# A fixed program order by kinds of matmul, and a new slot check, in a two-layer graph network on one core

## The chip, the core and the metric

The kernel runs on one core of a Trainium2 chip. The core has a matrix engine (PE; its weight loads are listed as PEld), a vector engine (DVE), a scalar engine (ACT), a general engine (POOL) and a queue that starts transfers (SP). Each engine executes its own instructions in the order in which the program issued them, and waits where one needs another engine's result or a buffer that is still read. The metric is the device time of one execution in microseconds (us); less is better.

## What is computed

128 graphs of 128 nodes with 64 features go through two layers, each followed by a residual sum and a layer norm. The reference, cut to what matters:

```python
def layer0(x, adj, W1, b1, W2, b2):          # W1 is 128 x 192, W2 is 192 x 64
    mask = (adj > 0.0)
    diff = x[:, :, None, :] - x[:, None, :, :]
    h = relu((x @ W1[:64])[:, :, None, :] + diff @ W1[64:] + b1)
    hm = einsum('bjkh,bjk->bjh', h, mask)    # sum over the neighbours k of j
    return hm @ W2 + mask.sum(-1)[..., None] * b2

def layer1(feat, adj, W1, b1, W2, b2, W3, b3):
    agg = einsum('bmn,bnd->bmd', adj, feat)
    return elu(elu(agg @ W1 + b1) @ W2 + b2) @ W3 + b3

x = layernorm(x + layer0(x, adj, ...))
x = layernorm(x + layer1(x, adj, ...))
```

The adjacency has few neighbours per node, so layer 0 visits neighbours and not all pairs of nodes.

## The kernel before

Graphs are handled in 64 pairs. In each pair the nodes are sorted by their number of neighbours. The sorted nodes fall into nine BLOCKS (first row, last row, slots): the 18 nodes of rows 65 to 83, for instance, get 9 slots each, which makes 162 columns. A node of block i must not have more neighbours than the block has slots; a check at the end of the kernel (overflow, L792) finds pairs for which that fails, and a dense path then does them again. For this input no pair needs it.

For each pair the work is a set of threads, Python generators whose every step names an engine, a cost, what it waits for, and how many of four shared PSUM banks (m0 to m3) it takes:

- prepare (L527): count the neighbours (DVE L536), make keys (POOL), spread them over rows (PE L549, L551), compare and rank (DVE L558), build a permutation (DVE L565).
- turn (L674): transpose adj and x (PE L680, L681) into one bank, copy it out as turned (ACT L685). project_c (L690) multiplies by weights (PE L698, L701) and splits the result into three bf16 parts cp (ACT, DVE L712, ACT L715, POOL L717).
- sort_x (L574) and project_a: sort x (PE L582), copy (ACT L586), multiply (PE L596), add the bias (ACT L603, gives aj), and a correction for short nodes: POOL L610, PE L616 and L619 (short), DVE L625, POOL L632.
- sort_mask (L635): sort the mask (PE L641, L644), copy it (ACT L649 mtp, L651 permT), count along a row (PE L655, prefix; ACT L658), and compare with slot numbers in nine pieces (DVE L665), which gives oh.
- unit, nine for a pair: copy aj into an edge bank (ACT L882; four edge banks e0 to e3, taken in turn), gather with 18 matmuls of a 64-column stationary side (PE L894), reduce over slots (DVE L903, gives sums).
- finish (L805): take off the correction (POOL L812, gives hm), project (PE L817, L821, L824), copy as ys (ACT L828), a small transfer of the degrees ys[128:130] to degs (SP L830), unsort (PE L836), norm, aggregate over neighbours (PE L843, ACT L847), hidden1 (PE L852), elu, hidden2 (PE L858), elu, last (PE L863, L865), norm, transfer out.

The class Flow (L88) writes the program order. It keeps a clock for each engine, and takes again and again the step that could start first; among steps of that engine that could start nearly as early (NEAR, NEAR_PE) it takes the one with the earliest due time. Due times are written out in DUE, relative to the start of a pair's round (ROUND times the pair's number). A step has a mode behind a colon: "PE:t" is work whose stationary side has 64 columns. A change of mode costs SWITCH on Flow's clock. Flow's clock only decides the order; it is no time of the chip. A unit also may not start, on that clock, before T0 + pace(u).

So the order of a period comes out of a list of dues and a rule that looks at readiness, and repeats itself from pair to pair once it has settled: one period of PE has nine gathers (L894) in five groups, and between them the steps of other pairs' threads.

Of the kernel before, what the change touches and what calls it, by code (L numbers as in the profile page):

```python
# [87 lines left out]
class Flow:  # L88
# [8 lines left out]

    LAG = 0.2
    NEAR = 0.1
    NEAR_PE = 0.03  # L100
    SWITCH = 0.1
    HOLD = 0

    def __init__(self, banks):
        self.clock = {}
        self.threads = []
        self.free = [(0.0, b) for b in banks]
        self.serial = 0
        self.mode = ""

# [35 lines left out]

    def _switch(self, engine, mode):
        return self.SWITCH if engine == "PE" and mode != self.mode else 0.0

    def _rank(self, th):  # L150
        engine, _, mode = th[4][0].partition(":")
        return th[0] + (self.HOLD if self._switch(engine, mode) else 0.0), th[1]

    def run(self):
        while self.threads:
            ready = [(t, th) for t, th in ((self._ready(th[4]), th) for th in self.threads)
                     if t is not None]
            t, th = min(ready, key=lambda r: (r[0], r[1][0], r[1][1]))
            first = th[4][0].split()[0].partition(":")[0]
            near = t + (self.NEAR_PE if first == "PE" else self.NEAR)  # L160
            t, th = min((r for r in ready if r[1][4][0].split()[0].partition(":")[0] == first
                         and r[0] <= near), key=lambda r: self._rank(r[1]))
            engine, cost, after, banks, fn = th[4]
            args = []
            if banks:
                self.free.sort(key=lambda f: f[0])
                args = [self.free.pop(0)[1] for _ in range(banks)]
            fn(*args)
            for e in engine.split():
                e, _, mode = e.partition(":")  # L170
                self.clock[e] = t + cost
                if e == "PE":
                    self.mode = mode
# [3 lines left out]
def sparse(tc, env):  # L177
# [6 lines left out]
    NE = 4  # L184
# [7 lines left out]
    ROUND = 11.14  # L192
    AHEAD = 3
    PACE = ROUND / NB

    DUE = {
        "prepare": (-34.32, -34.43, -29.25, -33.33, -26.26),
        "sort_x": (-25.05, -19.47, -20.79, -15.63, -11.78, -14.33, -11.15, -5.27, -5.97),
        "sort_mask": (-24.98, -24.21, -19.11, -17.63, -31.08, -14.67, -12.13, -9.2, -7.19, -6.42,
                      -4.21, -1.99, -12.24, -7.24),  # L200
        "turn": (-25.52, -21.42),
        "project_c": (-19.53, -25.02, -26.5, -19.03, -18.18, -16.73, -23.86),
        "finish": (7.83, 15.84, 19.72, 16.78, 21.09, 22.6, 28.99, 31.57, 29.07, 31.37, 30.6,
                   34.42, 35.7, 33.91, 37.94, 41.34, 41.72, 43.55, 44, 37.02, 51.36),
        "unit": (-1.1, 0.98, 2.36),
    }

    def pace(u):
        return PACE * u

    def begin_thread(name, p, gen):
        flow.start(ROUND * p, DUE[name], gen)

    T0 = []
# [17 lines left out]
    def pool(n):  # L232
        return 0.15 + n * 0.0022

# [31 lines left out]
    slots = const([P, 1], F32, "slots")  # L266
# [27 lines left out]
    worst = const([P, NP], F32, "worst")  # L294
    bad = const([P, NP], BF16, "bad")
    count = const([1, NP], I32, "count")
    some = const([1, 1], I32, "some")
    K = dict(count=count, some=some, ident=ident, identb=identb, onesb=onesb, mhalf=mhalf, mone=mone, slots=slots,
# [170 lines left out]
    def consts_late():  # L469
# [9 lines left out]
        def v1diag():  # L479
# [5 lines left out]
        ev, t = yield ("PE", 0.1, made("srow2", "small"), 1, lambda t: nc.tensor.matmul(  # L485
            t[:, :1], srow2, small[:, 0:1], start=True, stop=True))
        ev, = yield ("ACT", 0.2, [ev], 0, lambda: nc.scalar.copy(slots, t[:, :1]))
        flow.give(t, ev)


# [36 lines left out]
    def prepare(p):  # L527
# [4 lines left out]
        deg = prep.tile([P, 2], F32, name="deg")  # L532
# [12 lines left out]
        ev, = yield ("POOL PORT", 0.43, [ev] + made("jcol"), 0, keys)  # L545

        def spread(key):
            for s in range(2):
                nc.tensor.matmul(key[:, s * N:(s + 1) * N], degb[:, s:s + 1].to_broadcast([P, P]),  # L549
                                 identb, start=True, stop=True)  # L550
            nc.tensor.matmul(key[:, 2 * N:3 * N], small, iotb, start=True, stop=True)  # L551
        ev, key = yield ("PE", 0.17, [ev] + made("identb", "small", "iotb"), 1, spread)
# [37 lines left out]
    def project_a(p, xsT, ev):  # L590
# [19 lines left out]
        evs, = yield ("POOL PORT", 0.95, [have] + made("srow"), 0, lambda: nc.gpsimd.tensor_mul(sa, aj, srow))  # L610
# [24 lines left out]
    def sort_mask(p, ev):  # L635
# [3 lines left out]
        def sort(t):  # L639
            for s in range(2):  # L640
                nc.tensor.matmul(t[:, s * N:(s + 1) * N], d["mk"][:, s, :], permb[:, s, :],  # L641
                                 start=True, stop=True)
            for s in range(2):
                nc.tensor.matmul(t[:, (2 + s) * N:(3 + s) * N], permb[:, s, :], identb,  # L644
                                 start=True, stop=True)
        ev, t = yield ("PE", 0.22, [ev], 1, sort)
# [7 lines left out]
        ev, vps = yield ("PE", 0.11, [evm] + made("prefix"), 1,  # L654
                         lambda vps: nc.tensor.matmul(vps[:, :2 * N], prefix, flat(mtp),  # L655
                                                      start=True, stop=True))
# [17 lines left out]
    def turn(p):  # L674
# [7 lines left out]
        ev, t = yield ("PE", 0.4, [event("load", p)] + made("ident"), 1, transpose)  # L682
# [7 lines left out]
    def project_c(p, ev):  # L690
# [11 lines left out]
        ev, *cps = yield ("PE", 0.7, [ev] + made("wc", "b2p", "onesb"), 2, project)  # L702
# [19 lines left out]
    def norm(p, yps, ev, name, rest, shift):  # L722
# [29 lines left out]
        if p < LATE:  # L752
            ev, = yield ("POOL PORT", 1.24 if shift else 0.88, [ev] + made("mhalf"), 0, factors)
# [38 lines left out]
    def overflow(ev):  # L792

        v = nc.vector
        ev, = yield ("DVE", 0.25, [ev], 0, lambda: v.tensor_reduce(
# [352 lines left out]
```

## Time and profile before

| | us |
|---|---|
| Runs | 769.13 (median of 3), 766.89 to 770.3 |
| Profiled execution | 766.95 |
| Span of the profiled execution (first to last instruction) | 765.2 |
| PE busy, of the span | 746.0 |
| DVE busy | 718.6 |
| ACT busy | 700.9 |
| POOL busy | 430.7 |
| Gathers L894, 10368 matmuls | 390.8 |
| First reduce of the first pair | 23.90 after the start |
| Last reduce of the last pair starts | 746.00 after the start |

The costliest lines of the page beside the gathers are the reduces and the edge copies, each near 5 us for a pair, on DVE and on ACT:

```profile
L903 DVE TENSOR_REDUCE sums<-e 128x54 f32<-128x486 f32 (+8 forms) x576 | 330.5, 609 | 12.8 <-PE e L894 12.3
L882 ACT COPY e<-aj 128x504 f32<-128x504 f32 (+6 forms) x576 | 309.3, 558 | 7.2 <-DVE sums L903 6.8
```

A line of this kind names the line of code, the engine, the operation, output and input tiles with their shapes and the count; after the first bar stand the busy time in us and the mean of one in ns, after the second the idle time of the engine just before these instructions, and what ended most of it. Busy time on PE is not the same as work: matmuls are pipelined, and their ends are modelled. What one costs in a stream is the distance from its start to the next start.

### The profile page before, as it was taken

How to read it: one execution, taken by the hardware profiler on the slowest of the kernel's cores; microseconds unless marked ns; L12 is line 12 of the kernel's file. 1: busy time of each engine (PE TensorE's matmuls, PEld its weight loads, DVE VectorE, ACT ScalarE, POOL GpSimd, SP SyncE). 2: the span in 40 equal slices, each digit the busy share in tenths (PEclk: the TensorE clock that was granted, in tenths of full speed). 3: DMA queues.
4: the chain of work that ended last, by engine and by line, in shares of the span. 5: the costliest groups of instructions: out<-in, count | busy, mean ns of one | idle time of the engine just before them, and what ended most of it. 6: DMA issues, size and time to landing. Idle time of an engine off the chain costs nothing.

```text
span 765.2 us, 35336 instructions
## 1 busy us (share of the span) xinstructions
PE 746.0 (97%) x14487; PEld 671.7 (88%) x14488; DVE 718.6 (94%) x2363; ACT 700.9 (92%) x1987; POOL 430.7 (56%) x801
## 2 busy tenths in 40 slices
PE   7899999999999999999999999999999999999994
PEld 5688998998998999899899899899889889889893
DVE  7999999999999999999999999999999999999984
ACT  5788999999999999999999999999999999999984
POOL 6445565565665665665665665665665655655542
PEclk9999999999999999999999999999999999999998
DMA  3011110110110110110011010111011011010000
GB/s 82 3 24 27 28 30 21 27 31 19 28 30 20 28 29 21 26 31 23 25 30 27 21 31 22 26 31 30 18 31 30 18 31 31 17 30 21 9 10 18
DMA packets 63879, 19.73 MB, mean 26 GB/s; under 512 B 46816, under 2 KB 63712, under 8 KB 63712
## 3 DMA queue, kind: packets, MB, share of 16 engines
q1 hardware_dynamic: 63008, 17.12, 9.5%
q8 instruction: 115, 1.88, 1.0%
q14 instruction: 52, 0.43, 0.2%
q10 hardware_dynamic: 704, 0.30, 0.1%
HBM read 13.14 MB, written 4.19 MB: 23 GB/s over the span
## 4 chain that ended last, share of the span: by engine, by line
PE 94%; DVE 3%; ACT 2%; issue 1%; DMA 0%; ACTq 0%; POOLq 0%; POOL 0%; DVEq 0%
PE e L894 44%; PE m L596 6%; PE m L817 6%; PE m L698 5%; PE m L852 4%; PE m L858 4%; PE m L865 4%; PE m L836 3%; PE m L680 2%; PE m L582 2%; PE m L843 2%; PE m L655 2%; PE m L641 2%; PE m L821 1%; PE m L701 1%; DVE sums L903 1%
## 5 line engine op out<-in xcount | busy, mean ns | idle before, releaser
L894 PE MATMUL e<-oh,cp 128*64 128x162 bf16 (+3 forms) x10368 | 390.8, 228 | 1.8 <-ACT e L882 1.5
L894 PEld LDWEIGHTS <-cp 128*64 128x64 bf16 x10368 | 357.0, 110 | 30.6 <-issue 22.6
L903 DVE TENSOR_REDUCE sums<-e 128x54 f32<-128x486 f32 (+8 forms) x576 | 330.5, 609 | 12.8 <-PE e L894 12.3
L882 ACT COPY e<-aj 128x504 f32<-128x504 f32 (+6 forms) x576 | 309.3, 558 | 7.2 <-DVE sums L903 6.8
L665 DVE TENSOR_TENSOR oh<-vp,slotc 128x336 bf16<-128x336 bf16 (+6 forms) x576 | 168.5, 322 | 1.8 <-PE e L894 1.8
L610 POOL TENSOR_TENSOR sa<-aj,srow 128x384 f32<-128x384 f32 x64 | 65.0, 1016 | 121.0 <-ACT aj L603 118.7
L739 POOL TENSOR_SCALAR ve<-st 128x2 f32<-128x2 f32 x126 | 24.1, 192 | 160.2 <-DVE st L732 154.7
L740 POOL TENSOR_TENSOR rs<-ve,mhalf 128x2 f32<-128x2 f32 x126 | 87.6, 695 | 10.5
L717 POOL TENSOR_TENSOR cp<-r,cp 128x512 bf16<-128x512 f32 x64 | 74.1, 1158 | 13.2 <-ACT cp L715 13.2
L781 ACT ACTIVATE r<-m,cc 128x256 f32<-128x256 f32 x128 | 64.2, 502 | 4.9 <-PE m L852 3.9
L812 POOL TENSOR_TENSOR hm<-sums,corr 128x384 f32<-128x384 f32 x63 | 62.9, 999 | 8.0 <-DVE sums L903 8.0
L632 POOL TENSOR_TENSOR corr<-ea,sa 128x384 f32<-128x384 f32 x64 | 64.2, 1002 | 0.9 <-DVE ea L625 0.7
L787 DVE SCALAR_TENSOR_TENSOR h<-m,cc,e 128x256 f32<-128x256 f32 x128 | 61.1, 478 | 3.1 <-ACT e L784 3.1
L596 PE MATMUL m<-xsT,wad 128*128 128x128 f32 x384 | 58.4, 288 | 0.8 <-DVE r L712 0.6
L603 ACT ACTIVATE aj<-m,b1c 128x128 f32<-128x128 f32 x192 | 56.8, 373 | 1.0 <-PE m L596 1.0
L784 ACT ACTIVATE e<-r 128x256 f32<-128x256 f32 x128 | 57.6, 451 | 0.1
L761 ACT ACTIVATE x<-y,nb,rs 128x64 f32<-128x64 f32 x126 | 48.7, 434 | 9.1 <-POOL nb L743 8.8
L558 DVE SCALAR_TENSOR_TENSOR cmp<-m,keyc,tie 128x128 bf16<-128x128 f32 x128 | 39.9, 349 | 15.9 <-PE m L551 15.7
L817 PE MATMUL m<-w2d,hm 128*128 128x128 f32 x384 | 53.9, 277 | 0.0
L712 DVE TENSOR_TENSOR r<-m,cp 128x256 f32<-128x256 f32 x128 | 52.4, 413 | 0.8 <-ACT cp L708 0.7
L596 PEld LDWEIGHTS m<-xsT,wad 128*128 128x128 f32 x384 | 47.7, 191 | 1.9 <-DVE r L712 0.8
L817 PEld LDWEIGHTS m<-w2d,hm 128*128 128x128 f32 x384 | 48.6, 193 | 0.6
(150 smaller groups left out, 1349.5 us busy)
## 6 DMA issues: line engine op xcount, KB each, us to landing
adj<-in_adj_dram SPq DMA_DIRECT2D x64, 128.0 KB, 2.3
xx<-in_x_dram SPq DMA_DIRECT2D x64, 64.0 KB, 2.2
out_dram<-o SPq DMA_DIRECT2D x64, 64.0 KB, 1.7
degs<-ys SPq DMA_DIRECT2D x64, 1.0 KB, 1.7
w1s<-in_L_gnn_W_dram ACTq DMA_DIRECT2D x2, 96.0 KB, 2.9
w2s<-in_L_gnn_W_dram ACTq DMA_DIRECT2D x2, 48.0 KB, 2.5
v2s<-in_L_gnn_W_dram SPq DMA_DIRECT2D x1, 64.0 KB, 2.5
v1d<-in_L_gnn_W_dram SPq DMA_DIRECT2D x2, 32.0 KB, 2.1
```

What stands on the lines that cost most here:

```text
L596: nc.tensor.matmul(aps[:, c * N:(c + 1) * N], wad[:, c, :], xsT, start=True, stop=True)
L610: evs, = yield ("POOL PORT", 0.95, [have] + made("srow"), 0, lambda: nc.gpsimd.tensor_mul(sa, aj, srow))
L632: ev, = yield ("POOL PORT", 1.05, [ev, evs], 0, lambda: nc.gpsimd.tensor_sub(corr, ea, sa))
L665: lambda: nc.vector.tensor_tensor(oh[:, :, c].rearrange("p b (s w) -> p b s w", w=w), vp[:, :, p0:p1].rearrange("p b (o w) -> p b o w", o= ...
L717: lambda: nc.gpsimd.tensor_sub(cp[:, 2], r1, cp[:, 1]))
L740: nc.gpsimd.tensor_tensor(rs, ve, mhalf, op=OP.pow)
L781: lambda: nc.scalar.activation(r, z, AF.Relu, bias=c, scale=-1.0))
L812: lambda: (nc.vector if late else nc.gpsimd).tensor_sub(hm, d["sums"], d["corr"]))
L817: nc.tensor.matmul(yb[:, :2 * O], hm[:, c, :], flat(w2d[:, c]), start=(c == 0), stop=False)
L882: lambda: nc.scalar.copy(e.rearrange("p (c s w) -> p c s w", c=3, w=w), d["aj"][:, :, p0:p1].rearrange("p c (o w) -> p c o w", o=1) .to_br ...
L894: nc.tensor.matmul(e[s * HB:(s + 1) * HB, c * n:(c + 1) * n], cp[:, k, s, c * HB:(c + 1) * HB], oh[:, s, base:base + n], start=False, stop ...
L903: nc.vector.tensor_reduce(d["sums"][:, :, p0:p1], e.rearrange("p (c s w) -> p c w s", c=3, w=w), AX.X, OP.add, apply_absolute_value=True)
```

## The change

Five things are changed. A line number is that of the kernel before unless it is said otherwise; most lines of the changed kernel stand 9 to 30 lines further down.

1. *Flow* knows four kinds of matmul: "" (full array), "t" (64 columns), "r" (64 rows: L698) and "x" (transposes), and prices changes between them in a table. A kind "*" takes whatever kind is under way. From the first gather on until 14 units before the end (under_way) readiness is no longer looked at: the step with the earliest due time is next. The wait of units for T0 + pace(u) is gone.
2. *DUE* is new throughout: prepare is due 42.67 before its round and not 34.32, finish ends at 59.48 and not at 51.36, each of the nine units has dues of its own, ROUND is 11.1651. AHEAD is 4: a pair's inputs are loaded four rounds before its first unit and not three.
3. *stationary*: the matmuls of spread (L549, L551), of the sort of the mask (L641, L644) and of prefix (L655) are of kind "*". Under kind "t" each is issued as two with 64 columns of the stationary side.
4. *Degrees*: the counts of prepare go straight to degs; the two matmuls L824 for each pair, two columns of the copy ys and the transfer L830 are gone.
5. *overflow* compares the degrees with the slots of each block (nine compares), counts for each graph the rows over a limit (nine matmuls with one column of output) and compares those counts with the first row of the block. The matmul and copy that made slots (L485, L487) are gone.

In one period, PE now has four gathers (170, 162, 168, 66), project_c, last, then gather 112, short, gather 168, sort_x, gathers 154 and 169, the sort of the mask in halves, gather 154, aggregate, the transposes, spread, prefix, hidden2, project_a, project, hidden1, unsort. DVE has four reduces, elu, count, a sum, a reduce, ea, a reduce, two r, three reduces, cmp and permb, all nine compares of oh, a statistic, a sum, elu and a statistic. ACT has, between the gathers' edge copies, x, mtp, permT, agg, xsT, turned, vp in a row, then a copy, r, aj, ys, e. In the PSUM banks, the transposes and project_a of one period use the same bank (m3), with spread, prefix and hidden2 in the other three between them.

```diff
-    SWITCH = 0.1
-    HOLD = 0
+    CHANGE = {("t", ""): 0.1, ("", "t"): 0.1, ("r", "t"): 0.1, ("x", "t"): 0.1, ("", "r"): 0.1,
+              ("t", "r"): 0.1, ("x", "r"): 0.1, ("", "x"): 0.07, ("t", "x"): 0.1, ("r", "x"): 0.07}
...
+    def _kind(self, mode):
+        return mode if mode != "*" else "t" if self.mode == "t" else ""
+
     def _switch(self, engine, mode):
-        return self.SWITCH if engine == "PE" and mode != self.mode else 0.0
+        return self.CHANGE.get((self.mode, self._kind(mode)), 0.0) if engine == "PE" else 0.0
...
-            t, th = min(ready, key=lambda r: (r[0], r[1][0], r[1][1]))
-            first = th[4][0].split()[0].partition(":")[0]
-            near = t + (self.NEAR_PE if first == "PE" else self.NEAR)
-            t, th = min((r for r in ready if r[1][4][0].split()[0].partition(":")[0] == first
-                         and r[0] <= near), key=lambda r: self._rank(r[1]))
+            if self.under_way:
+                t, th = min(ready, key=lambda r: self._rank(r[1]))
+            else:
...
-    ROUND = 11.14
-    AHEAD = 3
-    PACE = ROUND / NB
+    ROUND = 11.1651
+    AHEAD = 4
...
+    def stationary(out, lhsT, rhs, **kw):
+
+        if flow.mode == "t":
+            for h in (slice(0, P // 2), slice(P // 2, P)):
+                nc.tensor.matmul(out[h], lhsT(h), rhs, **kw)
+        else:
+            nc.tensor.matmul(out, lhsT(slice(0, P)), rhs, **kw)
...
-        deg = prep.tile([P, 2], F32, name="deg")
+        deg = g.degs[:, 2 * p:2 * p + 2]
...
-        ev, key = yield ("PE", 0.17, [ev] + made("identb", "small", "iotb"), 1, spread)
+        ev, key = yield ("PE:*", 0.17, [ev] + made("identb", "small", "iotb"), 1, spread)
...
-                nc.tensor.matmul(t[:, s * N:(s + 1) * N], d["mk"][:, s, :], permb[:, s, :],
-                                 start=True, stop=True)
+                stationary(t[:, s * N:(s + 1) * N], lambda h: d["mk"][:, s, h], permb[:, s, :],
+                           start=True, stop=True)
...
-        ev, t = yield ("PE", 0.4, [event("load", p)] + made("ident"), 1, transpose)
+        ev, t = yield ("PE:x", 0.33, [event("load", p)] + made("ident"), 1, transpose)
...
-        ev, *cps = yield ("PE", 0.7, [ev] + made("wc", "b2p", "onesb"), 2, project)
+        ev, *cps = yield ("PE:r", 0.7, [ev] + made("wc", "b2p", "onesb"), 2, project)
...
+        def compare(blocks):
+            for i in blocks:
+                v.tensor_scalar(over[:, i, :], g.degs, float(BLOCKS[i][2]), None, op0=OP.is_gt)
+        for k in range(0, NB, 3):
+            ev, = yield ("DVE PORT", 0.5, [ev], 0, lambda: compare(range(k, k + 3)))
+
+        def rows_over(t):
+            for i in range(NB):
+                nc.tensor.matmul(t[:B, i:i + 1], over[:, i, :], onesb[:, 0:1], start=True, stop=True)
...
-            for s in range(2):
-                nc.tensor.matmul(yb[:, 2 * O + s:2 * O + s + 1], mtp[:, s, :], onesb[:, 0:1],
-                                 start=True, stop=True)
...
-        nc.sync.dma_start(g.degs[:, 2 * p:2 * p + 2], ys[:, 2 * O:])
...
+        flow.under_way = u < len(units) - 14
         ev, = yield ("PE:t", 0.03 + 0.0037 * n, [ev, event("cp", p), event("oh", p, i)], 0, gather)
```

## The prediction

> **What bounds the kernel now.** I read the busy times, then the stage windows, then the waits of the steady part, then one period of the timeline.
>
> ```profile
> PE 746.0 (97%) x14487; PEld 671.7 (88%) x14488; DVE 718.6 (94%) x2363; ACT 700.9 (92%) x1987; POOL 430.7 (56%) x801
> ...
> PE 94%; DVE 3%; ACT 2%; issue 1%; DMA 0%; ACTq 0%; POOLq 0%; POOL 0%; DVEq 0%
> ```
>
> Three engines look full. The windows say which one is:
>
> ```profile
> 300.00:400.00 100.00, 100.00 (x2004) 91.28 (x1998) 96.05 (x316) 95.41 (x273) 57.63 (x105) 1.00 0.11 27
> ```
>
> PE has no idle time in these 100 us, DVE and ACT have 4 to 5%. The waits between 150 and 700 us (48 periods) confirm it: no matmul is in the list as waiting for DVE, ACT or POOL, but those wait for PE. (Each line: who waits, for whom, total us, times, longest.)
>
> ```profile
> PEld L701 <- issue: 16.2, 49, 0.3
> PEld L894 <- issue: 16.2, 49, 0.3
> DVE cmp L558 <- PE m L551: 13.4, 49, 0.3
> ACT mtp L649 <- PE m L644: 11.4, 48, 0.2
> DVE sums L903 <- PE e L894: 9.4, 48, 0.2
> ```
>
> The two PEld lines are 0.3 us, once a period, in which no weights are loaded: the array changes its tiling. One period of the timeline, PE alone but for one line:
>
> ```profile
> 411.47 0.29 PE L641 MATMUL m<-permb,mk 128*128 128x128 bf16 x2
> ...
> 411.76 0.61 PE L865 MATMUL m<-v3s,h 128*128 128x64 f32 x4
> ...
> 412.30 0.70 PE L698 MATMUL m<-wc,turned 64*128 64x256 f32 x4
> ...
> 412.94 0.23 PE L701 MATMUL m<-b2p,onesb 128*128 128x64 bf16 x2
> ...
> 413.17 0.65 PE L858 MATMUL m<-h,v2s 128*128 128x256 f32 x2
> ...
> 413.75 1.48 PE L894 MATMUL e<-oh,cp 128*64 128x168 bf16 x36
> ...
> 417.66 0.91 PE L596 MATMUL m<-xsT,wad 128*128 128x128 f32 x6
> ...
> 422.90 0.28 PE L641 MATMUL m<-permb,mk 128*128 128x128 bf16 x2
> ```
>
> From L641 to L641 is 11.43 us; the first reduce of a pair comes every 11.432 us from pair 5 to pair 60. So the time is about 57 periods of 11.432 us, plus a head and a tail. The column after the tile names is the tiling: 128\*64 for gathers, 64\*128 for L698, 128\*128 otherwise.
>
> [...] L894 to L641: the last matmul of 112 columns needs 0.049 us, the next starts 0.146 us after it, so 0.097 for the drain. In the same way 0.093 at L865 to L698, 0.095 at L698 to L701, 0.093 at L858 to L894, 0.095 at L894 to L655 and 0.093 at L852 to L894. Transposes (L680) have the 128\*128 tiling: L596 to L680 costs nothing (0.112, its usual step). [...] Here an f32 load of 128 columns costs nothing behind a long matmul, but 0.104 after a drain (L817 at 724.71 took 0.377 instead of 0.275) or after a wait; 0.081 is left of it at L596, which follows the short matmuls L821 and L824.
>
> **The change on PE.** I laid the changed queue (its order is fixed by the program) out for one period, with start-to-start times of the same instructions in the trace. Gathers of 170, 162, 168 and 66 slots 0.688 + 0.634 + 0.652 + 0.285, drain 0.095: 2.35. project_c 0.70, last layer 0.056 + 0.540 with its drain: 3.65. Gather 112 0.487, short 0.112, 168 0.653, sort_x 0.247, 154 0.602, 169 0.660, sort as eight halves 0.222, 154 0.639, aggregate 0.218: 7.49. Drain 0.095, three transposes 0.327, their first load uncovered, which no row shows (0 to 0.104; their loads take 143 ns against 192, so I take 0.055): 7.97. spread 0.169, prefix 0.110, hidden2 0.432, project_a 0.670, project 0.844, hidden1 0.53, unsort 0.486 with its drain: 11.21. I take 11.2. The gain of 0.23 is one drain of six (0.095), the two degree matmuls L824 (0.054), weight loads that now follow a long matmul (0.08 at L596, 0.055 at L858, less 0.03 at hidden1), less the transposes' load. The halves cost nothing extra: two column tiles run side by side, as L616 and L619 do already (a pair every 0.056). Would they not, it were 0.22 a period.
>
> **New waits.** Without waits DVE needs 10.80 us a period (11.43 less gaps of 0.36 before cmp and 0.28 before a reduce) and ACT 10.65 (11.43 less gaps of 0.25, 0.26 and 0.27 before vp, x and mtp); neither becomes the bound. But every result that PE needs back within its full-array stretch is now close. Both ways are timed in the tail:
>
> ```profile
> 751.12 0.24 ACT L847 COPY agg<-m 128x128 f32<-128x128 f32 x1
> ...
> 751.41 0.71 PE L852 MATMUL m<-agg,v1p 128*128 128x128 f32 x4 [1.13 <-ACT agg L847]
> ```
>
> The copy ends at 751.357, PE resumes at 751.408 (0.051), with an uncovered load of 0.104. ACT starts 0.037 after a matmul's end (L649). *First place:* project_a writes the PSUM bank that the transposes filled, and waits for the copy turned (L685). From the last transpose's start: end 0.272, ACT 0.037, copy 0.47 to 0.51, back 0.051, load 0.104: 0.935. PE's work between is 0.109 + 0.169 + 0.110 + 0.432 = 0.82. Wait: 0.11. Before, L680 stood far from the next user of its bank, and the copy came 1.3 us after the transposes (418.63 and 419.91) without harm. *Second:* unsort waits for ys, with only hidden1 between. From project's last matmul 0.193 + 0.037 + 0.26 + 0.051 + 0.107 = 0.65; PE has 0.029 + 0.53. Wait: 0.09. Behind the waiting matmul stands everything on PE, and ACT's aj and ys copies and the next gathers' edges come later by as much. Together 0.20: period 11.40, gain 0.03, times 57 = 1.8 us. Bounds: the waits 0.05 (if the modelled ends are late) to 0.40 (if ACT itself is late there). ACT should not be: it still waits about 0.3 for the sort before mtp, permT, agg, xsT and turned. The edge copies have 0.4 us or more before their gathers, the reduces 0.8, though nine compares (2.07 us) now stand together on DVE; POOL's long operations fall outside them.
>
> **Head, tail, small edits.** Between 20 and 40 us DVE is busy 9.31 and 9.77 of 10 us: the head is bound by DVE. Ahead of the first reduce (23.90) its new queue has one count more (0.41), one pair of r (0.65), one compare (0.25) and the rows constants (2.9), and one ea less (0.46), so the first reduce comes at about 27.6; but none of it is extra work, and the later periods of the ramp are shorter by it. I take 0 +- 1.5. In the tail the slot check grows to nine compares (0.2 to 0.28 each by L401 and L536), beside the last pair's chain, mostly under POOL's power (DVE idle 0.80): 0 to 1.0, say 0.5. The drains that vanish there pay for it. The degs DMAs (64 x 0.47 us on SP) and the slots matmul were off the path: 0. The fifth early load on SP delays constants by about a microsecond, which the longer head covers. Sum: 766.95 (span 765.2 and 1.75 around it) - 1.8 = 765.1. The profiled execution lies 0.28% under the median of the runs, 769.13; on that footing 767.3.
>
> **Rivals.** *The waits are hidden* (0.05 or less): then 11.25 a period, 57 x 0.18 = 10.4 less, 758.7. For it: the chain uses modelled matmul ends. Against: the two handovers are each measured. *Slower: PE waits longer for ACT.* The point is 0.23 of waits a period, of which I see 0.20. ACT keeps one order, and once its 0.3 before mtp is used up, each delay goes to turned, project_a, aj, ys and unsort one for one. With waits of 0.40 the period is 11.60: 57 x 0.17 = 9.6 more, 778.7. For it: ACT is 95% busy, and a kept order can't go round a late copy. Against: its 10.65 us without waits. That the order doesn't do what it says is out: the changed queue repeats with every pair.
>
> **Numbers.** Half a percent (3.8 us) is what a measurement can tell from no change. Forecast 47% (761 to 772 alone), hidden 22%, slower 31%. The range 757.5 to 778 leaves out half of the hidden and the upper part of the slower case. Faster 0.25 (hidden and an edge of the forecast), same 0.42, slower 0.33.
>
> **What would show it.** Right: five gaps of the tiling a period instead of six; a wait of PE for ACT (turned) at project_a and one for ys at unsort, near 0.1 each, 64 times; first reduces 11.40 apart; no wait of PE in the gathers. Wrong: no PE wait and 11.2 apart (hidden), or PE waits for edge copies and 11.5 or more apart (slower), or the sort halves taking 0.44.

## The result, and the profile after

| | before | after |
|---|---|---|
| Median of 10 runs, us | 768.51 | 771.93 |
| Profiled execution | 766.95 | 772.32 |
| Its span | 765.2 | 770.6 |

The ratio is 1.0044, 95% interval 1.0032 to 1.0057: the changed kernel is slower, by 3.4 us of the median and 5.4 of the span. The forecast was 1.8 less. The time lies inside its range, on the wrong side of no change. The profiled run of the kernel before is one of the three fastest of its ten (766.89 to 766.97; the others took 768.38 to 770.3), so the two profiles lie some 2 us further apart than the medians.

The page of the changed kernel, busy times and the shares of the chain, looks like that of before:

```profile
PE 746.3 (97%) x14616; PEld 679.5 (88%) x14617; DVE 725.2 (94%) x2381; ACT 705.5 (92%) x1986; POOL 430.1 (56%) x801
...
PE 94%; DVE 3%; ACT 2%; issue 0%; DMA 0%; POOL 0%; ACTq 0%; POOLq 0%; DVEq 0%
```

So do the windows of its steady part (PE, PEld, DVE, ACT and POOL busy, then the granted clock of PE, the DMA share and GB/s):

```profile
300.00:400.00 100.00, 100.00 (x2026) 91.95 (x2026) 97.04 (x318) 96.53 (x273) 58.56 (x108) 1.00 0.11 27
```

The waits between 150 and 700 us (48 periods) hold one of the two that were expected: a wait of PE for turned at project_a (L606), once a period. A wait for ys at unsort is not in the list; the starts on PE, and e5 below, show it. (Each line: who waits, for whom, total us, times, longest.)

```profile
PEld L711 <- issue: 15.9, 48, 0.3
PEld m L606 <- ACT turned L695: 10.1, 49, 0.2
...
PEld m L690 <- issue: 8.2, 48, 0.2
ACT mtp L659 <- PE m L246: 7.8, 46, 0.2
DVE sums L930 <- PE m L629: 7.7, 39, 0.2
```

And one period of the timeline, PE alone, from the sort in halves (L246) to the first gathers of the next:

```profile
410.88 0.32 PE L246 MATMUL m<-permb,mk 128*64 128x128 bf16 x4
410.99 0.32 PE L246 MATMUL m<-identb,permb 128*64 128x128 bf16 x4
...
412.06 0.44 PE L690 MATMUL m<-ident,adj 128*128 128x128 f32 x2
...
412.72 0.65 PE L886 MATMUL m<-h,v2s 128*128 128x256 f32 x2
413.21 0.91 PE L606 MATMUL m<-xsT,wad 128*128 128x128 f32 x6
413.95 0.83 PE L847 MATMUL m<-w2d,hm 128*128 128x128 f32 x6
...
415.32 0.65 PE L864 MATMUL m<-ys,permT 128*128 128x64 f32 x4
415.90 2.44 PE L920 MATMUL e<-oh,cp 128*64 128x170 bf16 x72
...
423.46 0.44 PE L690 MATMUL m<-ident,adj 128*128 128x128 f32 x2
```

From L690 to L690 it is 11.40 here, 11.395 a pair in the mean: the forecast of a period was 11.40. The loss is elsewhere. The starts of the first reduce of a pair, pairs counted from 0, show where:

| us from the start | before | after | difference |
|---|---|---|---|
| pair 0 | 23.90 | 32.09 | +8.19 |
| pair 5 | 79.44 | 87.11 | +7.67 |
| pair 60 | 708.34 | 713.82 | +5.48 |
| pair 63 | 739.04 | 740.93 | +1.89 |
| end of the last reduce | 746.69 | 750.30 | +3.61 |
| end of the span | 765.19 | 770.58 | +5.39 |

So the head (all that stands ahead of pair 5) loses 7.67, 55 steady periods win 2.19 back (11.4345 to 11.3946 us each), pairs 60 to 62 another 3.59, the last pair's gathers lose 1.72, and what follows the last reduce loses 1.78. These sum to the 5.39 of the span. From pair 60 to the end both take the same, 56.8. The whole loss is the head's.

Windows of 10 us in the head (columns as above; the number behind x counts the instructions), first before, then after:

```profile
20.00:30.00 10.00, 9.10 (x159) 7.06 (x159) 9.31 (x32) 7.76 (x24) 5.25 (x6) 1.00 0.01 3
30.00:40.00 10.00, 8.54 (x190) 7.54 (x191) 9.77 (x32) 6.47 (x15) 4.24 (x7) 1.00 0.02 2
```

```profile
20.00:30.00 10.00, 4.54 (x17) 3.30 (x18) 7.61 (x31) 3.57 (x11) 2.11 (x2) 0.52 0.01 2
30.00:40.00 10.00, 8.15 (x158) 7.38 (x158) 5.99 (x14) 3.98 (x11) 1.16 (x1) 0.80 0.01 2
```

Two things are seen. PE does 17 matmuls where it did 159, and no engine is full: DVE, which was, is busy 7.61 and 5.99. And the granted clock of PE, 1.00 before, is at half: in windows of half a microsecond it is 0.50 from 20.5 to 34.0. In the kernel before, the timelines of PE and DVE show the first four gathers in a row and the first reduce behind the first of them:

```profile
22.27 2.23 PE L894 MATMUL e<-oh,cp 128*64 128x162 bf16 x72
...
23.90 0.65 DVE L903 TENSOR_REDUCE sums<-e 128x54 f32<-128x486 f32 x1
```

The timeline of the changed kernel shows why PE stands still:

```profile
19.87 0.76 DVE L722 TENSOR_TENSOR r<-m,cp 128x256 f32<-128x256 f32 x2 [1.33 <-ACT cp L718]
...
20.35 1.55 PE L708 MATMUL m<-wc,turned 64*128 64x256 f32 x4 [0.89 <-DVE r L722]
...
22.98 0.58 PE L504 MATMUL m<-onesf,v2s 128*128 128x1 f32 x2 [0.87 <-DVE r L722]
...
24.14 0.15 DVE L508 TENSOR_TENSOR cc<-cc,m 128x1 f32<-128x1 f32 x1 [0.88 <-PE m L505]
...
28.52 0.19 DVE L366 COPY rowp<-low 1x128 bf16<-1x128 bf16 x1
...
28.72 2.15 DVE L675 TENSOR_TENSOR oh<-vp,slotc 128x324 bf16<-128x324 bf16 x9
...
30.68 3.14 PE L920 MATMUL e<-oh,cp 128*64 128x162 bf16 x53 [4.92 <-DVE oh L675]
...
32.09 0.67 DVE L930 TENSOR_REDUCE sums<-e 128x54 f32<-128x486 f32 x1 [1.23 <-PE e L920]
```

From 24.14 to 28.71 DVE makes the late constants (consts_late: cc, means, rows, rowp), one short dependent step after another. Behind them in DVE's order stand nine compares oh (five of pair 1 and the last four of pair 0, in turn), and PE, which is at the first gather of pair 0, waits 4.92 for them. Strict order is in force from the first gather on, and looks at dues alone: the late constants were started with due -5.58, those compares are due -3.15 to -2.11. Work for later pairs stands ahead on PE as well: the project_c at 20.35 waits 0.89 for the two banks of the one before it, and the constants' product L504 behind it waits 0.87 for the same step of DVE (r, L722). In that project_c the four matmuls L708, which take 0.70 at full clock, take 1.55.

### The profile page after: what moved, and what is told of

Its sections match the earlier page's. It is cut to its first block, busy times and chain, and to the rows that moved or that the text cites. A ratio compares the mean times of both kernels' runs of the same rounds, so it can differ in the third digit from the quotient of the medians.

```text
span 770.6 us, 36007 instructions
## 1 busy us (share of the span) xinstructions
PE 746.3 (97%) x14616; PEld 679.5 (88%) x14617; DVE 725.2 (94%) x2381; ACT 705.5 (92%) x1986; POOL 430.1 (56%) x801
## 4 chain that ended last, share of the span: by engine, by line
PE 94%; DVE 3%; ACT 2%; issue 0%; DMA 0%; POOL 0%; ACTq 0%; POOLq 0%; DVEq 0%
PE e L920 45%; PE m L606 6%; PE m L708 5%; PE m L847 5%; PE m L880 4%; PE m L886 4%; PE m L864 4%; PE m L893 4%; PE m L690 3%; PE m L248 2%; PE m L871 2%; PE m L592 2%; PE m L246 2%; PE m L851 1%; PE m L711 1%; PE m L691 1%
## 5 line engine op out<-in xcount | busy, mean ns | idle before, releaser
L930 DVE TENSOR_REDUCE sums<-e 128x54 f32<-128x486 f32 (+8 forms) x576 | 327.1, 609 | 16.7 <-PE m L629 9.9
L910 ACT COPY e<-aj 128x504 f32<-128x504 f32 (+6 forms) x576 | 293.3, 540 | 9.5 <-DVE sums L930 8.9
L675 DVE TENSOR_TENSOR oh<-vp,slotc 128x308 bf16<-128x308 bf16 (+6 forms) x576 | 137.3, 314 | 0.8 <-ACT vp L668 0.6
L727 POOL TENSOR_TENSOR cp<-r,cp 128x512 bf16<-128x512 f32 x64 | 74.4, 1162 | 18.6 <-ACT cp L725 18.6
L791 ACT ACTIVATE r<-m,cc 128x256 f32<-128x256 f32 x128 | 61.3, 479 | 2.4 <-PE m L886 2.4
L606 PEld LDWEIGHTS m<-xsT,wad 128*128 128x128 f32 x384 | 48.3, 193 | 13.0 <-ACT turned L695 11.8
L606 PE MATMUL m<-xsT,wad 128*128 128x128 f32 x384 | 58.4, 289 | 0.6 <-DVE r L722 0.6
L794 ACT ACTIVATE e<-r 128x256 f32<-128x256 f32 x128 | 53.3, 418 | 2.0
L722 DVE TENSOR_TENSOR r<-m,cp 128x256 f32<-128x256 f32 x128 | 47.8, 415 | 2.8 <-ACT cp L718 2.8
L708 PE MATMUL m<-wc,turned 64*128 64x256 f32 x256 | 46.3, 436 | 0.9 <-DVE r L722 0.9
```

What stands on the lines that cost most here:

```text
L606: nc.tensor.matmul(aps[:, c * N:(c + 1) * N], wad[:, c, :], xsT, start=True, stop=True)
L675: lambda: nc.vector.tensor_tensor(oh[:, :, c].rearrange("p b (s w) -> p b s w", w=w), vp[:, :, p0:p1].rearrange("p b (o w) -> p b o w", o= ...
L708: nc.tensor.matmul(cps[s][:, :cols], d["turned"][k, 2, :], wc[k, :], start=True, stop=False)
L727: lambda: nc.gpsimd.tensor_sub(cp[:, 2], r1, cp[:, 1]))
L910: lambda: nc.scalar.copy(e.rearrange("p (c s w) -> p c s w", c=3, w=w), d["aj"][:, :, p0:p1].rearrange("p c (o w) -> p c o w", o=1) .to_br ...
L930: nc.vector.tensor_reduce(d["sums"][:, :, p0:p1], e.rearrange("p (c s w) -> p c w s", c=3, w=w), AX.X, OP.add, apply_absolute_value=True)
```

## The experiments

Every time is the median of the kernel's runs, the ratio is to the kernel before on the same chip, and "pair 5" is the first reduce of pair 5 in the profile (79.44 before, 87.11 after). Edits are against the changed kernel unless said otherwise. The theories: A, strict order in the head; B, the constants arrive late, behind the fifth pair's inputs; C, the slot check at the end.

**e1: strict order one pair later.**

```diff
-        flow.under_way = u < len(units) - 14
+        flow.under_way = 9 <= u < len(units) - 14
```

> Strict order begins with the gathers of the second pair instead of with the first gather; the later periods are untouched. Theory A (the loss sits in the head, because strict order puts every overdue step of DVE ahead of the first pair's one-hot compares): the first reduce moves from 32.1 us to 24 to 28, part of that is given back when the overdue steps come in the second pair, and the time is 766 to 770 (ratio to before 0.997 to 1.002). Theory B (the constants land later, because a fifth pair is loaded ahead of them): the first reduce stays within 1 us of 32.1 and the time at 771 to 773. Theory C (the grown slot check at the end): also 771 to 773, with the first reduce anywhere.

Measured: 772.68, ratio 1.0041 (1.0028 to 1.0054). The first reduce came at 21.40, earlier than before's 23.90, and nothing of it was kept: pair 1 began at 44.02 (after: 43.99), pair 5 at 88.04. In the timeline of e1 PE meets the same kind of wait a pair later:

```profile
35.91 1.22 PE L708 MATMUL m<-wc,turned 64*128 64x256 f32 x2 [4.73 <-DVE ea L635]
```

A project_c that is overdue has gone first and waits for a bank that ea is to free, while DVE has other overdue steps, nine compares among them, ahead of ea. Theory A as it was put falls: it is not the moment at which strict order begins. What stays is the second half of it: at whatever moment it begins, steps that the dues want early stand ahead of those that PE needs now. The clock fell to 0.50 here too, from 33.5 on.

**e2: the late constants spread out.**

```diff
-    flow.start(ROUND * -0.5, [0.0], consts_late())
+    flow.start(ROUND, [1.1 * k for k in range(28)], consts_late())
```

> Only the ranks of the late constants change: their steps (4.6 us of DVE in one chain, two products on PE) are spread over the second to fourth pair instead of standing together ahead of the first pair's compares. Theory A: the first reduce comes at 26 to 29 instead of 32.1, and the time is 766 to 769.5 (ratio 0.997 to 1.002), period unchanged at 11.39. If it is rather the three pairs of project_c, each waiting for the two banks of the one before, that hold the compares: first reduce within 1.5 us of 32.1, time 770.5 to 772.5. Theory B (constants land later): the late constants no longer stand ahead of anything, so this would also help; the run e3 tells A from B.

Measured: 768.2, ratio 0.999 (0.9982 to 0.9998), as expected of A: first reduce at 26.50, pair 5 at 83.99, period 11.3946 as before the edit. So 3.1 of the 7.67 is the place of these steps in the order, of DVE above all (their two products on PE moved with them). But the clock is still halved; the window of e2:

```profile
20.00:30.00 10.00, 7.96 (x83) 5.90 (x83) 5.90 (x17) 4.47 (x13) 1.17 (x1) 0.50 0.01 1
```

PE is busy 7.96 and gets 83 matmuls done, where before 9.10 was enough for 159.

**e3: the constants loaded after the first pair.**

```diff
         if p == 0:
             arrive_next()
+            arrive_late()
...
-    arrive_late()
     flow.run()
```

> The late constants are loaded right after the first pair instead of after the fifth; the order on PE, DVE, ACT and POOL is unchanged. Theory B: the chain that waited for them starts earlier, the first reduce moves from 32.1 to 29 or less, time 766 to 770. Theory A: the constants were in time, the first reduce stays at 31.5 to 33, time 771 to 773.

Measured: 771.15, ratio 1.0028 (1.0017 to 1.0039); first reduce 31.82, pair 5 at 86.33. Theory B is out as the main cause. That pair 5 is 0.8 earlier says little: e8 and e11 below have the same order in the head, and in their profiles pair 5 comes at 81.46 and 82.48.

**e4: no slot check.** The body of overflow becomes two memsets of its results.

> The slot check is left out: its two results are set to zero, so nothing counts rows that have too many ones. Theory A: the tail alone gets shorter, by 0.4 to 1.2 us, so 770.7 to 771.6 (ratio 1.003 to 1.004). Theory C (the nine compares and two products stand in the last pair's chain and are what is lost): 3 us or more less, 769 or below.

Measured: 770.4, ratio 1.0013 (1.0005 to 1.0022), span 768.4: 2.2 less, all of it behind the last reduce (18.08 instead of 20.28). That is more than A allowed and less than C claimed. The two timelines, first the changed kernel, then e4 (its L861 is L886, its L868 is L893):

```profile
755.76 0.48 DVE L797 SCALAR_TENSOR_TENSOR h<-m,cc,e 128x256 f32<-128x256 f32 x1 [0.71 <-ACT e L794]
...
756.16 0.49 DVE L816 TENSOR_SCALAR slotc<-degs 128x128 bf16<-128x128 f32 x3
...
756.56 0.53 DVE L760 TENSOR_SCALAR x<-y,st,rs 128x64 f32<-128x64 f32 x2
...
761.11 1.22 PE L886 MATMUL m<-h,v2s 128*128 128x256 f32 x2 [0.48 <-DVE h L797]
...
763.86 1.12 PE L893 MATMUL m<-v3s,h 128*128 128x64 f32 x4 [1.42 <-DVE h L797]
```

```profile
755.80 0.54 DVE L760 TENSOR_SCALAR x<-y,st,rs 128x64 f32<-128x64 f32 x2 [1.52 <-POOL rs L767]
...
756.25 0.48 DVE L797 SCALAR_TENSOR_TENSOR h<-m,cc,e 128x256 f32<-128x256 f32 x1
...
759.64 0.70 PE L861 MATMUL m<-h,v2s 128*128 128x256 f32 x2 [0.56 <-DVE h L797]
...
762.05 0.75 PE L868 MATMUL m<-v3s,h 128*128 128x64 f32 x4 [0.72 <-DVE h L797]
```

In the changed kernel three compares and an h stand ahead of the last pair's x on DVE; in e4 that h comes behind it. So x is 0.76 later, and by hidden2 it is 1.47. The rest goes with the clock: in the changed kernel it falls to 0.50 at 761.1, and hidden2 and last take 1.22 and 1.12; in e4 it falls at 762.5, behind the starts of both, and they take 0.70 and 0.75.

**e5: project ahead of project_a.** This tests the two waits that the prediction saw in the steady part.

```diff
-        "sort_x": (..., -13.03, -12.9, 2.76, ...),
-        "finish": (12.51, 20.73, 21.24, ...),
+        "sort_x": (..., -12.68, -12.63, 2.76, ...),
+        "finish": (12.51, 20.73, 20.79, ...),
```

> The ranks of project_a and its copy aj are moved behind project and its copy ys; nothing else is changed. In the steady part PE then runs hidden2, project, project_a, hidden1, unsort, so that 1.2 us of PE work (project_a and hidden1) stand between project and unsort instead of 0.53. Theory D (the steady part is PE's work of 11.2 us, plus 0.1 to 0.2 for turned and 0.09 for ys, each a wait of its own): the ys wait goes, the turned wait stays and is now seen at project; period 11.29 to 11.33 instead of 11.395, time 766 to 768.5. Rival E (ACT is the limit here, and a copy that is late in one place is late in the next): period 11.38 or more, time 771 to 774.

Measured: 790.32, ratio 1.0264 (1.0246 to 1.0282), period 11.62: 18 us slower than the changed kernel, outside the ranges of D and of E. By starts on PE the gain that D expected is there: from unsort to the first gather 0.487 instead of 0.580, so the ys wait was 0.093. But the first gathers behind it take 2.68 instead of 2.36. The waits of e5 from 150 to 700 us say what is new:

```profile
ACT aj L613 <- PE m L606: 23.3, 48, 0.5
...
PEld L920 <- issue: 11.7, 47, 0.3
```

ACT stands still 0.49 a period ahead of aj, until PE has made project_a, and with it everything behind: elu's exponential and the edge copies of the next gathers. The mechanism of rival E acts in this place: ACT waits longer, and its kept order hands the delay on. The periods account for 12.4 of the 15.8 by which the span grew; behind the last reduce it takes 25.0 instead of 20.3, and why stays open.

**e7: the sort of the mask on the full array.**

```diff
-        if flow.mode == "t":
+        if False:
```

> The sort products between the gathers use the full array again (four matmuls of 128x128 instead of eight halves), with the order of the queue kept. Theory F (the gain of the steady part is tilings saved, about 0.095 a change): two changes more in each period, 0.19 less the 0.00 to 0.05 that halves cost, so a period of 11.54 to 11.60 and 781 to 784. Rival G (a change of tiling among short matmuls is hidden by waits that are there anyway): period under 11.45, time under 775.

Measured: 786.01, ratio 1.0211 (1.0194 to 1.0227), period 11.640. That is 0.245 a period more than in halves, and above the 0.19 of the forecast's upper case: by starts on PE 0.141 where the gathers end and 0.104 where the sort ends. Rival G is out: nothing hides these two changes of tiling. Theory F has the cause and its sign, but its price of 0.095 a change is too low here; what makes up the other 0.055 stays open.

**e8: e2 with more matmuls in the head.** Sixteen matmuls that write again what the edge banks hold, in three places of the head where PE would wait anyway.

```diff
+    def warm(n):
+        for t in edges[1:1 + n]:
+            for k in range(2):
+                nc.tensor.matmul(t[:, 2 * k * P:2 * (k + 1) * P], identb, onesb,
+                                 start=(k == 0), stop=(k == 1))
...
+            if p == 1:
+                warm(2)
...
+            if p == 1:
+                warm(3)
...
+            if p == 2:
+                warm(3)
```

(The three places are sort_x, project_a and project_c.)

> The kernel of e2 (late constants spread) with 16 extra matmuls in three places of the head where PE waited 0.5 to 0.9 us: they write again what the edge banks hold already, and nothing waits for them but the first edge copies. In e2 the granted clock of PE was 0.50 from about 20 to 30 us. Theory H (the halved clock is the second part of the loss in the head, worth about 3 us): the clock stays at 0.9 or above from 20 to 30 us, the first reduce of the sixth pair comes at 80 to 82 us instead of 84.0, time 764.5 to 767. Rival I (PE was waiting for DVE and ACT anyway, the clock cost nothing): the sixth pair at 83.5 to 85, time 768 to 770, even with the clock at 1.00. If the clock drops all the same, the run tells nothing of either.

Measured: 765.93, ratio 0.9952 (0.9938 to 0.9966); pair 5 at 81.46. The window of e8, to be held against that of e2:

```profile
20.00:30.00 10.00, 7.33 (x138) 5.77 (x138) 8.04 (x22) 6.65 (x18) 1.99 (x2) 1.00 0.01 3
```

Extra work made it 2.3 us faster than e2. Theory H holds: the clock is 1.00 here and was 0.50 in e2, and the halved clock is the second part of the loss in the head, 2.5 us by pair 5.

**e9: e2, e5's ranks and an early slot check together.** The check has a buffer of its own and its steps are spread over the four periods ahead of the end.

> Three edits together: the late constants spread (e2), project ahead of project_a (e5), and the slot check made as soon as the last pair's rows are counted, in a buffer of its own, spread over the four periods before the end (for which one of fourteen input buffers is given up). From the parts: 3.7 us less by e2, 3 to 6 by e5 if theory D holds, 1 to 2.2 by the check (leaving it out took 1.5 us off the median and 2.2 off the span): 760 to 764, ratio 0.989 to 0.994. With rival E: 766 to 768.

Measured: 783.67, ratio 1.0188 (1.0172 to 1.0204). The period is e5's, 11.62, and the forecast falls with theory D. From the first reduce of pair 60 to the end it took 59.7 against e5's 61.5: 18.6 instead of 25.0 behind the last reduce, but 41.1 instead of 36.5 ahead of it. So most of what the early check saved at the end was lost in the four periods where its steps then stood; through which engine is not shown.

**e10: e8 with project first, and aj behind the exponential.** What e5 lacked: ACT gets work for the time in which it would wait.

```diff
-        "sort_x": (..., -13.03, -12.9, 2.76, ...),
-        "finish": (12.51, 20.73, 21.24, ...),
+        "sort_x": (..., -12.68, -11.83, 2.76, ...),
+        "finish": (12.51, 20.73, 20.79, ...),
```

> The kernel of e8 with project ahead of project_a as in e5, but on ACT aj now stands behind the exponential of hidden2 as well, so that ACT has that to do while PE makes project_a. e5 showed the ys wait gone (0.093 a period less at unsort) and 0.32 more at the first gathers behind it, with ACT idle 0.49 ahead of aj. Theory J (in e5 the idle time of ACT made the edge copies behind aj late): ACT's idle time ahead of aj falls to 0.1 to 0.25 a period, the first gathers take 2.36 to 2.45 again, the period is 11.28 to 11.34 and the time 760 to 763. Rival K (the gathers were held by the edge copies because aj itself, 0.85, now stands nearer to them, whatever ACT waits for): period 11.45 or more, time 769 or more.

Measured: 762.69, ratio 0.9908 (0.9892 to 0.9923), period 11.309. The waits of e10:

```profile
PEld m L859 <- ACT turned L705: 10.0, 48, 0.2
...
ACT aj L623 <- PE m L616: 8.1, 48, 0.2
```

ACT's wait is 0.17 a period, the first gathers take 2.37 again, unsort stays at 0.487. Theory J holds: the order on ACT, not the move on PE, had cost e5 its time. The wait for turned is still there, now at project.

**e11: e8 with the compares placed otherwise.** Two groups behind the last pair's ve, the third behind its x.

```diff
-            ev, = yield ("DVE PORT", 0.5, [ev], 0, lambda: compare(range(k, k + 3)))
+            ev, = yield ("DVE PORT", 0.5, [ev, event("tail", k == NB - 3)], 0, lambda: compare(range(k, k + 3)))
...
             ev, = yield ("DVE", 0.1, [ev], 0, variance)
+            if shift:
+                happened([ev[0] - flow.LAG], "tail", False)
...
             ev, = yield ("DVE", 0.4, [ev], 0, lambda: [center(s) for s in range(2)])
+            happened([ev[0] - flow.LAG], "tail", True)
```

> The kernel of e8 with the slot check's compares placed differently on DVE in the tail: the first three and next three only after the last pair's ve, the last three after its x. Nothing is left out. Theory L (two groups of compares stand in front of the last pair's norm, 0.4 to 0.8 us of the 2.2 that leaving the check out saves; the rest comes from the order and the clock behind): 0.4 to 1.5 us less than e8, 764.4 to 765.5. Rival (the cost of the check is in its two products and the reductions behind them): within 0.3 of e8's 765.9.

Measured: 765.91, ratio 0.9959 (0.9943 to 0.9974), no less than e8, so theory L's 0.4 to 1.5 did not come, and the time is where the rival had it. In the profiles it is 19.37 from the last reduce to the end against e8's 19.73. Where the 1.5 to 2.2 of the check could be saved without leaving it out stays open.

**e12: e10 and e11 together.**

> e10 and e11 together. If theories J and L hold, their sum: 758.5 to 762, ratio 0.986 to 0.992; with K 769 or more.

Measured: 763.12, ratio 0.9918 (0.9904 to 0.9932): e10's time again, 1.1 above the range, in which L's part was counted.

**e13: the pieces of oh laid apart.** By now the head's 4.92 had a second reading. The piece that the first gather reads was made by 15.97; its second matmul starts at 30.68, and the last piece of pair 0 ends at 30.62. That matmul waits for a semaphore of DVE, and by the times it is this last piece that ends the wait. Only the layout of the tile is changed, and no order.

```diff
-                             oh[:, :, c].rearrange("p b (s w) -> p b s w", w=w),
+                             oh.rearrange("p b e -> p (b e)")[:, 2 * base:2 * (base + n)]
+                             .rearrange("p (b s w) -> p b s w", b=2, w=w),
...
-                                         oh[:, s, base:base + n],
+                                         flat(oh)[:, 2 * base + s * n:2 * base + (s + 1) * n],
```

> The changed kernel with another layout of the tile oh: each of its nine pieces lies in one stretch (both graphs of a piece together) instead of in two, half a tile apart. The order of all engines stays. In the changed kernel the second matmul of the first gather waits until the last piece of pair 0 is made (it starts 0.05 us after that), though its own piece was ready at 15.97: the stretches of pieces with two halves overlap. Theory M: with pieces apart that wait of 4.92 goes, the first four gathers run from about 25.4 us, the first reduce still comes behind the nine compares on DVE (30.5 to 31.3), pair 5 comes at 84 to 86 instead of 87.1, and the time is 768.5 to 771. Rival N (the edge banks are held by reduces that stand behind the compares anyway): pair 5 within 0.8 of 87.1, time 771 to 772.5.

Measured: 766.17, ratio 0.9963 (0.9948 to 0.9978), 5.8 less than the changed kernel and faster than the kernel before. The timeline of e13:

```profile
25.05 2.81 PE L921 MATMUL e<-oh,cp 128*64 128x162 bf16 x54
...
30.41 1.93 DVE L931 TENSOR_REDUCE sums<-e 128x54 f32<-128x486 f32 x4
...
31.79 0.84 PE L921 MATMUL e<-oh,cp 128*64 128x168 bf16 x18 [2.57 <-ACT e L911]
```

Three gathers run while DVE makes the constants and a fourth (28.59) while it makes the compares; what PE waits for then is an edge bank, behind the first reduce (30.41). Pair 5 begins at 84.64, 2.5 earlier. The clock is at half from 20.1 to 26.9, and again from 33.8 to 37.2, behind that wait. Theory M holds for the head: the first gather had been waiting 4.92 for pieces that it doesn't read. The time is below its range all the same, since the head was less than half of what e13 won. More came from something in nobody's theory: the period is 11.338 instead of 11.395, 3.1 us over 55 pairs (more on it at the end).

**e14: e10 with e13's layout.**

> e10 with the layout of e13. In e8, whose head e10 has, the first gathers still waited 1.97 for the compares. Theory M: 0.5 to 2 us less than e10, 760.7 to 762.2, ratio 0.988 to 0.990. Rival N: 762.2 to 763.5.

Measured: 759.83, ratio 0.9882 (0.9868 to 0.9897), 2.9 less than the median of e10 and better than theory M said. But the runs of e10 spread with the clock in the head (see the end): against its two with a mean clock of 0.996, 761.23 and 761.45, e14 wins 1.4 to 1.6, which is within M's 0.5 to 2. Its window, to be held against the two of before:

```profile
20.00:30.00 10.00, 8.58 (x172) 7.01 (x171) 9.05 (x25) 7.37 (x20) 3.21 (x3) 1.00 0.02 4
```

PE gets 172 matmuls done there, before 159. Pair 5 begins at 79.65, 0.2 behind the kernel before, so the head's loss is made good, and the period is 11.312. This is the best version found, 12 us below the changed kernel and 8.7 below the one before.

## Why the prediction was wrong

**The change on PE: right.** The sum of 11.2 without waits stands: 11.395 less the waits below is 11.18. Halves cost 0.223 as put, and e7 prices the two changes of tiling that they save at 0.245. What the prediction calls a drain is the 0.093 to 0.097 that the starts lose at a change of tiling; what PE does in that time no trace shows. (The list of what makes up the gain of 0.23 adds up to 0.20 only; the row of starts, on which the forecast rests, is not touched by that.)

**New waits: right, place and size.** For turned 0.11 was put. By starts, hidden2 to project_a takes 0.486 instead of 0.432 and project_a 0.740 instead of 0.670, 0.124 together; no run takes this wait away, so its size rests on the starts alone. For ys 0.09 was put, and e5 measured 0.093. The rival "hidden" is out. The slower rival, PE waiting longer for ACT, did not occur in the changed kernel, but e5 shows its mechanism in the same stretch: 0.49 of ACT's time a period was enough for 11.62. The 1.8 us for 57 periods are 2.2 for 55 in the profile.

**Head: here it failed.** The step reads "the head is bound by DVE", its additions put the first reduce "at about 27.6; but none of it is extra work, and the later periods of the ramp are shorter by it. I take 0 +- 1.5." The first reduce came at 32.09, 8.19 later than before and not 3.7, and little of that was given back: at pair 5 7.67 were still missing. Four things are wrong in the step. DVE's busy time in the kernel before was carried over to a queue in another order: with strict order DVE is busy 7.61 and 5.99 of 10, since it waits in turn for ACT and PE (1.06 for cp ahead of r at 22.51, 0.88 for PE at 24.14, 1.23 at 32.09). A step that is moved ahead was priced at its own length, but in a kept order it also holds everything behind it: 4.6 of constants in front of the compares gave PE a wait of 4.92. Which compares the gather really waits for was not asked: a tile's pieces were taken one by one, while the first gather went on only behind the last piece of pair 0 (30.62 and 30.68), and with the pieces apart started at 25.05 (e13). And PE, which waits more, had half its clock from 20.5 to 34.0 us, for which the sum had no term.

The size can be split. Up to pair 5 PE's idle time in the timeline is 13.20, and 7.51 before: 5.7 more. In the stretch at half clock it waited 5.8, so it was busy for some 7.7; by an estimate from the granted clock, 0.50 and not 1.00, that would have been half as long at full clock: 3.9 less. That is 9.6, 1.9 more than was lost: ends of matmuls are modelled, and the two heads do not hold quite the same work by then, so the split is rough. The runs say the same from the other side: the place of the constants 3.1 (e2), the clock 2.5 (e8), and with the pieces apart and the order of e10 as well 0.2 remain (e14). e13 alone takes 2.5 off; it and e2 work on the same wait, so these don't add up.

**Tail.** "0 to 1.0, say 0.5" for the slot check was 2.2 of the span. The compares were priced where they stand (0.49 for three) and x was 0.76 later, as an h had also come ahead of it; what was left out is that order, the order behind it and the clock. That pairs 60 to 62 pass 3.6 us faster than before was not foreseen either, and no run tells why; it and the losses of the last pair cancel. That the time still lies inside 757.5 to 778 is luck: the upper part of that range was kept for longer waits in the steady part, which did not occur.

## What to carry to other kernels

An order found for the steady part needs a beginning of its own: dues that are right for a running pipeline put late constants, work for later pairs and all writers of a tile ahead of what the first gather needs, and a wait may then cover more than its instruction reads (4.92 for a piece made by 15.97, in e13 gone). In a kept order the price of a moved step is what waits behind it on its engine, so a change of PE's order can need one of ACT's with it (e5 and e10: 11.62 and 11.31 a period). Where PE is partly idle, read its granted clock together with its waits (here it fell to 0.50 behind ten us in which PE was busy 7.68).

## What was not expected of the hardware

In the changed kernel PE's clock fell to 0.50 at 20.4, with no gap of PE above 0.9 us in the ten before it, in which PE was busy 7.68. It was back at 34.0, 3.3 after the gathers had begun at 30.68. What makes it fall the runs don't tell, and the busy time of ten us alone does not decide it: in e12 PE was busy 7.32 from 20 to 30 us and in e8 7.33, and the clock was 1.00 there and in the ten us behind. The stretches at half clock are 13.65 us long in the head of the changed kernel, 10.2 in that of e2 (20.0 to 30.2) and 6.8 and 3.4 in that of e13: four, three, two and one times 3.41.

The clock also differs from run to run. e10 and e12 have the same order of instructions in the head, and in the profiles the clock from 20 to 30 us was 0.83 in one and 1.00 in the other; pair 5 came at 83.29 and 80.88. That is the same effect as in e8, without an edit that touches the head. The six runs of e10 spread accordingly, 761.23 with a mean granted clock of 0.996 to 764.14 with 0.992. So does the kernel before: of its 41 runs beside e1, the five with a mean clock of 0.996 took 766.91 to 767.14, the 18 with 0.991 769.06 to 770.75.

The shorter period of e13 comes above all from the gathers of 154 columns. The 18 matmuls of a gather belong to the two graphs in turn. In the changed kernel those of one graph start every 66.6 ns and those of the other every 69.3; with e13's layout it is 66.6 and 66.7. From one gather to the next nothing is won (154 to 169 takes 0.600 in both): the lag of the one graph is carried on (at the start of 169 it is 42 ns, with e13's layout 3). It is paid where a row of gathers ends: from the last 154 to aggregate 0.600 instead of 0.622, from there to the transposes 0.321 instead of 0.335; the four first gathers take 2.347 instead of 2.364. That is 0.053 of the 0.057. The operands are the same but for where the second graph's half begins. Why it matters was not tried. In e14 the period is the same as in e10 (11.312 and 11.309): the last 154 takes 0.600 there too, but the step from aggregate to the transposes takes 0.380 instead of 0.335, so what is won is lost again in front of the transposes.
